# Scores' maxima placed behind the reciprocals of two Sinkhorn chains in VectorE's instruction order

## The chip, the core and the metric

The kernel runs on one core of a Trainium2 chip. The engines are TensorE (PE, with its weight loads shown apart as PEld), VectorE (DVE), ScalarE (ACT), GpSimd (POOL) and SyncE (SP, which issues the DMAs). Each of them takes its own instructions strictly in the order of its own list, and an instruction that waits holds up all that stand behind it in the same list. The metric is the device time of one execution in microseconds: before the change the median of three runs is 1359.68 us (1355.14 to 1362.71).

## The reference, cut to what matters

Two transformer layers with adaptive layer norm. The first (gated linear attention and a binarised feed-forward) fills about the first 900 us and is not touched. The second layer is a softmax attention (batch 2, 512 tokens each, 32 heads of 16), and then a feed-forward made of four streams, whose mixing matrices come from 50 rounds of a Sinkhorn normalisation for each of 1024 tokens:

```python
scores = einsum('bqhd,bkhd->bhqk', q, k) / sqrt(D)
probs  = softmax(scores)                       # needs a row's maximum
out    = einsum('bhqk,bkhd->bqhd', probs, v)
...
Z = (x_norm @ W_res.T + H_res_base) / tau      # a 4 x 4 matrix for each token
for _ in range(50):
    u = -logsumexp(Z + v[None, :], axis=-1)
    v = -logsumexp(Z + u[:, None], axis=-2)
H_res = exp(Z + u[:, None] + v[None, :])
...
x_mixed = einsum('btij,btjc->btic', H_res, x_streams)
```

## The kernel before

Tokens lie on the 128 partitions, so there are eight tiles of 128 tokens: four of batch 0 and four of batch 1.

**The attention of the second layer** is cut into 16 steps (batch, half of the queries, group of heads) of 8 pieces each. `piece()` emits, for one piece, `maxima(order[i], k)`, then the weighing of a piece that lies ten behind, then `aside(2)`. `maxima` writes two score tiles: a matmul (L880) into one of three PSUM banks, and a VectorE reduction (L884) that takes the negated maximum of each row and so frees the bank. That makes 256 maxima in all; they are counted here as maximum 1 to 256. After every four pieces the eight maxima are split in two parts (L894 on ScalarE, L895 on GpSimd), transposed, and sent into the queries' tile. `weigh` repeats the scores with the maxima subtracted (L918) and takes the exponential on ScalarE (tile `pt`, L78). `outputs` (L938) and `finish` (reciprocal L964, product L966 on VectorE, addition L972 on GpSimd) close one "quad" for every eight maxima.

**The Sinkhorn chains** are generators that `aside` advances two steps for each piece. As soon as two token tiles of the attention's output are complete, a chain begins:

- chain a (`streams0(0)`, tiles 0 and 1 of batch 0) and chain b (`streams0(2)`, tiles 2 and 3 of batch 0): 49 iterations each, whose products and sums run on GpSimd and whose reciprocals run on VectorE;
- the chain of batch 1, whose products, sums and reciprocals are all on VectorE (`last` is true): 16 iterations of the first two tiles alone, 33 of all four tiles together (the joint chain, 128x16 operands), and 16 of the last two tiles alone.

One half iteration of chain a or b is a round between two engines: a product on GpSimd (L1183 or L1187), two additions on GpSimd (L1176, L1177), a reciprocal on VectorE (L1185 or L1189), and then the product of the next half. At iterations 16 and 32 the kernel matrix is renewed from logarithms, with ScalarE in the round (L1193, L1166, L1167). `opening` comes before a chain (statistics, two products per tile on GpSimd for batch 0 in L1061 and L1062), `mixed_on_tensor` after it (diagonal matrices `dg` on ScalarE, matmuls L1236, product `fout` L1210 on VectorE, addition L1211 on GpSimd).

**The order of the lists** is made by a list scheduler from the dependencies and priorities, when the program is built; the text of the kernel gives only the dependencies. The kernel also adds dependencies that cost no semaphore and only fix the order of two instructions of one engine:

```python
order_only = mybir.DependencyInfo(mybir.DependencyClass.NoSync, mybir.DependencyReason.DATA)
tc.add_manual_dep(m, i.name, order_only, reason="the work beside keeps its place")
```

In the list built for VectorE before the change, 64 of chain a's 98 reciprocals and 28 of chain b's 98 stand ahead of maximum 256; the other 104 stand behind it.

Of the kernel before, what the change touches and what calls it, by code (L numbers as in the profile page):

```python
# [52 lines left out]
def tile_adaln(ctx: ExitStack, tc: tile.TileContext, a: dict, out: bass.AP):  # L53
    nc = tc.nc
# [22 lines left out]
    def act(o, i, func, **kw):  # L77
        ins = nc.scalar.activation(o, i, func, **kw)  # L78
        tc.add_manual_dep(
            ins.ins, table.ins.name,  # L80
            mybir.DependencyInfo(mybir.DependencyClass.NoSync, mybir.DependencyReason.DATA),
            reason="the activation table",
        )
        return ins.ins
# [52 lines left out]
    anchor = {}  # L137
    order_only = mybir.DependencyInfo(mybir.DependencyClass.NoSync, mybir.DependencyReason.DATA)
# [32 lines left out]
    def temp(shape, dt, name, bufs=2):  # L171
        return wk.tile(shape, dt, name=name, bufs=bufs)
# [642 lines left out]
    def key_tile(i):  # L815
        return i % 2 if i < TWO else (i - TWO + 2) % 3
# [54 lines left out]
    def maxima(st, k):  # L871

        assert holder[key_tile(st["i"])] == st["i"]
        rp, j = divmod(k, 4)
        s, i = divmod(j, 2)
        if j == 0:
            st["m"] = small.tile([P, NQ * 2, 2], FP, name="m")
        for qt in range(NQ):
            ps = psp.tile([P, L], FP, name="s1", bufs=S1)
            anchor["pe"] = nc.tensor.matmul(  # L880
                ps, lhsT=st["qs"][rp][0:KS, i, qt * P:(qt + 1) * P], rhs=st["ks"][s][0:KS],
                start=True, stop=True,
            ).ins
            anchor["dve"] = nc.vector.tensor_reduce(  # L884
                st["m"][:, 2 * qt + s, i:i + 1], ps, AX.X, ALU.max, negate=True
            ).ins
        if j == 3:
            m2 = small.tile([P, NQ * 2, 2, 2], FR, name="m2")
            hi, lo = m2[:, :, 0], m2[:, :, 1]
            if st is order[-1]:  # L890
                nc.vector.tensor_copy(hi, st["m"])
                nc.vector.tensor_tensor(lo, st["m"], hi.bitcast(FP), ALU.subtract)
            else:
                nc.scalar.copy(hi, st["m"])  # L894
                nc.gpsimd.tensor_tensor(lo, st["m"], hi.bitcast(FP), ALU.subtract)  # L895
            mt = psp.tile([8, Q], FP, name="mt", bufs=MT)
            for qt in range(NQ):
                nc.tensor.transpose(
                    mt[:, qt * P:(qt + 1) * P],
                    m2[:, 2 * qt:2 * qt + 2].bitcast(FP).rearrange("p a b c -> p (a b c)"), ident,  # L900
                )
            mm = temp([8, L], FR, "mm")[:, 0:Q]
            nc.scalar.copy(mm, mt)
            anchor["sp"] = nc.sync.dma_start(out=st["qs"][rp].bitcast(FP)[96:100], in_=mm.bitcast(FP)).ins

    def weigh(st, k):

        assert holder[key_tile(st["i"])] == st["i"]
        rp, r = divmod(k, 4)
        kp, s = divmod(r, 2)  # L910
        if r == 0:
            quads.append({"st": st, "rp": rp, "pt": {}})
        qd = quads[-1]
        for i in range(2):
            ps = psp.tile([P, 2, Q], FP, name="s2", bufs=S2)
            for j in range(2):
                kt = 2 * kp + j
                nc.tensor.matmul(  # L918
                    ps[:, j, :], lhsT=st["ks"][s][0:KM, kt * P:(kt + 1) * P], rhs=st["qs"][rp][0:KM, i, :],
                    start=True, stop=True,  # L920
                )
            p = wts.tile([P, 2, Q], FP, name="pt", bufs=PT)
            anchor["act"] = qd["last"] = act(p, ps, AF.Exp, scale=0.25)
            qd["pt"][2 * s + i, kp] = p

    quads = []

# [232 lines left out]
    def iterations(R, its, renew, last):  # L1160

        z, t, K, u, v, fa, fb, fl = (R[k] for k in ("z", "t", "K", "u", "v", "fa", "fb", "fl"))
        big = nc.vector if last else nc.gpsimd

        def kernel_of():
            nc.vector.tensor_tensor(K, z, over(u), ALU.add)  # L1166
            nc.vector.tensor_tensor(K, K, along(v), ALU.add)  # L1167
            act(K, K, AF.Exp)

        def sums(dst, y):  # L1170

            if last:
                nc.vector.tensor_reduce(dst, y, AX.X, ALU.add)  # L1173
            else:
                h2 = R["pairs"]
                nc.gpsimd.tensor_tensor(h2, y[:, :, :, 0:2], y[:, :, :, 2:4], ALU.add)  # L1176
                nc.gpsimd.tensor_tensor(dst, h2[:, :, :, 0], h2[:, :, :, 1], ALU.add)  # L1177

        for it in its:
            if it == 1 or it - 1 in renew:  # L1180
                sums(fa, K)
            else:
                big.tensor_tensor(t, K, along(fb), ALU.mult)  # L1183
                sums(fa, t)
            nc.vector.reciprocal(fa, fa)  # L1185
            yield
            big.tensor_tensor(t, tp_(K), along(fa), ALU.mult)  # L1187
            sums(fb, t)
            nc.vector.reciprocal(fb, fb)  # L1189
            if it in renew:  # L1190
                for d, f in ((u, fa), (v, fb)):
                    act(fl, f, AF.Ln)
                    nc.vector.tensor_tensor(d, d, fl, ALU.add)  # L1193
                kernel_of()
            yield
# [70 lines left out]
    def streams0(c0):  # L1266

        S = {"b": 0, "c0": c0, "n": 2}
        yield from opening(S, False)
        R = chain_room(2, False)  # L1270
        yield from first_iteration(S, R)
        yield from S["branch"]
        yield from iterations(R, range(1, NITER), RENEW, False)
        result(S, R)
        for c in range(2):
            yield from mixed_on_tensor(S, c, nc.gpsimd)
# [3 lines left out]
    def streams1a():  # L1280

        S = joint["a"] = {"b": 1, "c0": 0, "n": 2}
        yield from opening(S, True)
        R = joint["R"] = chain_room(4, True)
        yield from first_iteration(S, part(R, 0, 2))
        yield from S["branch"]
        yield from iterations(part(R, 0, 2), range(1, HEAD + 1), (HEAD,), True)

    def streams1b(ahead):
# [16 lines left out]

        side.append((1, branches(), UP))
        yield from iterations(R, range(1, NITER - HEAD), RENEW, True)
        result(A, part(R, 0, 2))
        side.append((None, mixed_on_tensor(A, 0, nc.gpsimd), UP))  # L1310
# [44 lines left out]
    def piece():  # L1355
        p = at[0]
        at[0] += 1
        if p == 0:
            begin()
        i, k = divmod(p, 8)  # L1360
        if k == 0 and i < len(order):
            load_step(i + 1)
        if p < n_pieces:
            maxima(order[i], k)
        if wt[0] <= p - slack(p):
            weighed()
        if k == 4 and i + 1 < len(order):
            keys1(i + 1)
        with tc.high_priority(UP):
            if p >= HOLD and p % POP == 0 and virtual:  # L1370
                tail(virtual.pop(0))
        aside(2)
# [3 lines left out]
    def weighed():  # L1376
        w = wt[0]
        wt[0] += 1
        if w < n_pieces:
            if w == n_pieces // 2:  # L1380
                values1(1)
            weigh(order[w // 8], w % 8)
        o = w - OUT
        if 0 <= o < n_pieces and o % 4 == 3:
            outputs(o // 4)
        o -= 5
        if o >= 0 and o % 4 == 0 and o < n_pieces:
            j = o // 4
            finish(j)
            if j % 16 == 5:  # L1390
                with behind():
                    row_tiles(j // 16, (SB, CB, GB))
                    weights24(j // 16)
            if j % 8 == 7:
                k = j // 8
                if k == 2:
                    joint["ahead"] = streams1a()
                side.append((RATES[k], (streams0(2 * k) if k < 2 else joint["ahead"] if k == 2 else streams1b(joint["ahead"])), UPS[k]))
# [40 lines left out]
    for n, u in enumerate(units):  # L1439
        g, b, c = u["at"]  # L1440
        s = n // NC
# [127 lines left out]
```

## Time and profile before

| What | Value |
|---|---|
| Median of three runs | 1359.68 us |
| The profiled execution, its own time | 1362.77 us |
| Its span in the trace | 1361.1 us |
| PE busy | 1236.3 us (91%) |
| DVE busy | 1098.5 us (81%) |
| ACT busy | 845.2 us (62%) |
| POOL busy | 788.3 us (58%) |
| Maximum 96, 192, 224 and 256 end at | 1057.5, 1165.3, 1195.4 and 1225.1 us |
| First reciprocal of chain a | 1081.1 us |
| Last addition of the attention's output (L966 of the last quad) | 1241 us |
| Joint chain, first and last reciprocal | 1256.2 and 1320.6 us |

An engine's busy share is an average over stages that have different limits. Three stages matter here: the attention while the chains run beside it (1081 to 1225 us), the rest of the attention with the openings of the last tiles (1225 to 1256 us), and the tail in which the chains alone are left (1256 to 1361 us).

### The profile page before, as it was taken

Reading aid. Unit: us, or ns where it says so; the run is one execution under the profiler, and the core shown is the slowest. Engines: PE = TensorE matmul, PEld = TensorE weight load, DVE = VectorE, ACT = ScalarE, POOL = GpSimd, SP = SyncE. Lnnn points to the kernel's source line nnn. Section 1 sums busy time; section 2 is a strip of 40 time slices with the busy share of each in tenths; the row PEclk is TensorE's granted clock in tenths of the full one; section 3 lists DMA queues with packets and bytes.
Section 4 is the critical chain, followed back from the end, with each engine's and each line's share of the span. In section 5 each row is a group of like instructions: output and inputs, shape, how many; then the busy total and the mean of one; then the engine's idle time right before and its main releaser. Section 6 shows DMA issues by size and latency. Waiting matters only on the chain. (4 is left out here: it accounts for less than half of the span.)

```text
span 1361.1 us, 23047 instructions
## 1 busy us (share of the span) xinstructions
PE 1236.3 (91%) x7216; PEld 996.9 (73%) x7216; DVE 1098.5 (81%) x2668; ACT 845.2 (62%) x2380; POOL 788.3 (58%) x1235
## 2 busy tenths in 40 slices
PE   6889999999999999999989999898999999995408
PEld 3677888788788778888877787676777777764308
DVE  7897678787686687877989887867878888898888
ACT  4565476476466566766657675566667678775417
POOL 5353374365266357776788878444444755668751
PEclk9999999999999999999999999998998999997659
DMA  8111341231132142333343233424203221200001
GB/s 255 57 57 32 97 121 40 71 109 55 46 95 93 54 139 95 86 108 93 101 125 109 82 113 91 127 71 132 81 28 116 81 68 50 66 14 2 9 8 47
DMA packets 69762, 109.68 MB, mean 81 GB/s; under 512 B 13436, under 2 KB 20348, under 8 KB 69640
## 3 DMA queue, kind: packets, MB, share of 16 engines
q1 hardware_dynamic: 69640, 108.21, 26.9%
q8 instruction: 57, 0.93, 0.3%
q14 instruction: 65, 0.53, 0.1%
HBM read 99.89 MB, written 8.02 MB: 79 GB/s over the span
## 5 line engine op out<-in xcount | busy, mean ns | idle before, releaser
L884 DVE TENSOR_REDUCE m<-s 128x1 f32<-128x512 f32 x256 | 165.7, 670 | 13.6 <-PE s L880 13.0
L78 ACT ACTIVATE pt<-s 128x512 f32<-128x512 f32 x256 | 137.6, 600 | 13.4 <-PE s L918 12.6
L78 ACT ACTIVATE sg<-sg 128x512 f32<-128x512 f32 x128 | 80.8, 632 | 57.9 <-DVE sg L512 56.0
L481 POOL TENSOR_TENSOR q<-xcos,rot 128x512 f32<-128x512 f32 x64 | 92.9, 1452 | 39.7 <-DVE xcos L479 36.9
L880 PE MATMUL s<-ks,qs 96*128 96x512 f32 x256 | 105.1, 438 | 8.4 <-DVE m L884 6.2
L251 PE MATMUL pps<-hh,wq_h 128*128 128x512 f32 x256 | 102.0, 399 | 0.9 <-DVE zl L605 0.9
L78 ACT ACTIVATE dec<-dec,room 128x128 f32<-128x128 f32 x256 | 82.7, 398 | 32.1 <-POOL dec L529 31.9
L529 POOL TENSOR_SCALAR_AFFINE_SELECT dec<-gb 128x512 f32<-128x512 f32 x64 | 47.1, 736 | 95.6 <-DMA gb<-g_dram 35.1
L251 PE MATMUL ops<-wo_h,zh 128*128 128x512 f32 x256 | 101.3, 396 | 0.9 <-DVE zl L605 0.9
L251 PE MATMUL ops<-wo_h,zl 128*128 128x512 f32 x256 | 100.8, 394 | 0.9 <-DVE zl L605 0.9
L251 PE MATMUL gps<-wg_h,hh 128*128 128x512 f32 x256 | 101.1, 395 | 0.0
L251 PE MATMUL gps<-wg_l,hh 128*128 128x512 f32 x256 | 101.0, 394 | 0.0
L918 PE MATMUL s<-qs,ks 100*128 100x256 f32 x512 | 99.3, 301 | 1.7 <-ACT pt L78 1.2
L251 PE MATMUL gps<-wg_h,hl 128*128 128x512 f32 x256 | 100.6, 393 | 0.0
L251 PE MATMUL pps<-hl,wq_h 128*128 128x512 f32 x256 | 100.3, 392 | 0.0
L251 PE MATMUL ops<-wo_l,zh 128*128 128x512 f32 x256 | 100.1, 391 | 0.0
L251 PE MATMUL pps<-hh,wq_l 128*128 128x512 f32 x256 | 100.1, 391 | 0.0
L549 POOL TENSOR_TENSOR gb<-gb,q 128x512 f32<-128x512 f32 x48 | 63.2, 1318 | 63.1 <-ACT gb L78 52.2
L582 PE MATMUL yps<-v,dec 128*128 128x128 f32 x512 | 93.8, 278 | 3.8 <-DVE xcos L479 2.8
L918 PEld LDWEIGHTS s<-qs,ks 100*128 100x128 f32 x512 | 83.0, 195 | 18.0 <-ACT pt L78 5.3
L592 DVE SCALAR_TENSOR_TENSOR z<-yps,ss,sg 128x128 f32<-128x128 f32 x256 | 71.8, 341 | 28.4 <-ACT ss L78 28.1
L556 POOL TENSOR_TENSOR xw<-v,room 128x512 f32<-128x512 f32 x48 | 55.5, 1171 | 60.4 <-ACT v L496 58.1
(327 smaller groups left out, 3924.5 us busy)
## 6 DMA issues: line engine op xcount, KB each, us to landing
gb<-g_dram SPq DMA_DIRECT2D x64, 256.0 KB
raw<-in_wq SPq DMA_DIRECT2D x56, 256.0 KB
raw<-in_wg SPq DMA_DIRECT2D x48, 256.0 KB
raw<-in_wo SPq DMA_DIRECT2D x48, 256.0 KB
raw<-in_wmod SPq DMA_DIRECT2D x40, 256.0 KB
qs<-q_dram SPq DMA_DIRECT2D x64, 64.0 KB
raw<-in_wk SPq DMA_DIRECT2D x14, 256.0 KB
raw<-in_wv SPq DMA_DIRECT2D x14, 256.0 KB
```

The costliest lines, as they stand in the source:

```text
L78: ins = nc.scalar.activation(o, i, func, **kw)
L251: nc.tensor.matmul(ps, lhsT=l, rhs=r, start=i == 0, stop=i == n - 1)
L481: nc.gpsimd.tensor_tensor(dst, sp(xc_), sp(rot), ALU.add)
L529: anchor["pool"] = nc.gpsimd.affine_select(out=dec, in_=gb, pattern=[[0, REP0], [1, P]], compare_op=ALU.is_ge, fill=-1e30, base=0, channel ...
L549: nc.gpsimd.tensor_tensor(gb, gb, q[:, c], ALU.mult)
L556: nc.gpsimd.tensor_tensor(xw, u["v"][:, c, :].unsqueeze(1).to_broadcast(sh4), wdc[:, c, r0:r0 + REP0].unsqueeze(2).to_broadcast(sh4), ALU. ...
L582: nc.tensor.matmul(yps[:, h, :], lhsT=u["pr"][:, h, :], rhs=u["v"][:, c, :], start=True, stop=not c)
L592: nc.vector.scalar_tensor_tensor(z[:, h, :], yps[:, h, :], ss[:, h:h + 1], sg[:, h * P:(h + 1) * P], ALU.mult, ALU.mult)
L880: anchor["pe"] = nc.tensor.matmul(ps, lhsT=st["qs"][rp][0:KS, i, qt * P:(qt + 1) * P], rhs=st["ks"][s][0:KS], start=True, stop=True,).ins
L884: anchor["dve"] = nc.vector.tensor_reduce(st["m"][:, 2 * qt + s, i:i + 1], ps, AX.X, ALU.max, negate=True).ins
L918: nc.tensor.matmul(ps[:, j, :], lhsT=st["ks"][s][0:KM, kt * P:(kt + 1) * P], rhs=st["qs"][rp][0:KM, i, :], start=True, stop=True,)
```

## The change

Every reciprocal of chains a and b is noted in a queue of its chain when it is emitted. Every maximum, when it is emitted, is given an order-only dependency on the oldest noted reciprocal of a chain: maxima of odd number on that of the oldest chain that has any left, maxima of even number on that of each of the first two chains that have any left. The chain of batch 1 is not noted. No instruction is added or removed, and no semaphore.

```diff
@@ maxima @@
             anchor["dve"] = nc.vector.tensor_reduce(
                 st["m"][:, 2 * qt + s, i:i + 1], ps, AX.X, ALU.max, negate=True
             ).ins
+            pace(anchor["dve"])
...
+    paced = {}
+    turn_ = [0]
+
+    def pace(m):
+
+
+        turn_[0] += 1
+        for q in [q for q in paced.values() if q][:1 if turn_[0] % 2 else 2]:
+            tc.add_manual_dep(m, q.pop(0).name, order_only, reason="the chain's reciprocals keep pace")
...
@@ iterations @@
-            nc.vector.reciprocal(fa, fa)
+            r = nc.vector.reciprocal(fa, fa).ins
+            if not last:
+                paced.setdefault(id(R), []).append(r)
             yield
             big.tensor_tensor(t, tp_(K), along(fa), ALU.mult)
             sums(fb, t)
-            nc.vector.reciprocal(fb, fb)
+            r = nc.vector.reciprocal(fb, fb).ins
+            if not last:
+                paced[id(R)].append(r)
```

## The prediction

> **What bounds the kernel now.** I read the slices of the page first, then the engines' busy time by stretch, then the maxima alone by stretch, and last the order of time around the chains.
>
> ```profile
> PE   6889999999999999999989999898999999995408
> DVE  7897678787686687877989887867878888898888
> ```
>
> PE is full until slice 36 and half empty after it: there is an attention that PE fills, and a tail in which it hardly works.
>
> ```profile
> core 0: us, PE busy (x) PEld busy (x) DVE busy (x) ACT busy (x) POOL busy (x), PEclk, DMA share, GB/s
> 1081.00:1165.00 84.00, 81.69 (x727) 62.19 (x728) 73.69 (x208) 68.56 (x168) 50.16 (x166) 0.96 0.24 64
> 1165.00:1195.00 30.00, 30.00 (x283) 23.11 (x281) 25.46 (x77) 22.54 (x56) 21.51 (x94) 1.00 0.27 62
> 1195.00:1225.00 30.00, 29.35 (x263) 20.33 (x267) 28.76 (x106) 23.35 (x60) 17.32 (x81) 1.00 0.04 10
> 1225.00:1256.00 31.00, 17.18 (x171) 12.60 (x162) 27.24 (x180) 16.93 (x50) 25.48 (x115) 0.81 0.01 2
> 1256.00:1321.00 65.00, 16.69 (x96) 15.33 (x95) 56.03 (x282) 17.01 (x62) 43.13 (x196) 0.61 0.02 9
> ```
>
> From 1081 to 1225 us PE is the bound (141 of 144 us) with VectorE close behind; from 1256 us on VectorE is (56 of 65 us), working on the joint chain, which reads tiles that the attention completes last.
>
> ```profile
> core 0: us, DVE busy (x), PEclk, DMA share, GB/s
> 1081.00:1165.00 84.00, 57.69 (x90) 0.96 0.24 64
> 1165.00:1195.00 30.00, 20.39 (x33) 1.00 0.27 62
> 1195.00:1225.00 30.00, 21.19 (x33) 1.00 0.04 10
> ```
>
> These are the maxima alone: 0.93, 0.91 and 0.91 us for each. That pace is to be compared with the chains' own.
>
> ```profile
> 1313.34 0.25 POOL L1187 TENSOR_TENSOR sinkhorn<-sinkhorn 128x32 f32<-128x32 f32 x1 [0.32 <-DVE sinkhorn L1185]
> 1313.67 0.22 POOL L1176 TENSOR_TENSOR sinkhorn<-sinkhorn 128x16 f32<-128x16 f32 x1
> 1313.96 0.20 POOL L1177 TENSOR_TENSOR sinkhorn<-sinkhorn 128x8 f32<-128x8 f32 x1
> 1314.48 0.24 POOL L1183 TENSOR_TENSOR sinkhorn<-sinkhorn 128x32 f32<-128x32 f32 x1 [0.32 <-DVE sinkhorn L1189]
> ```
>
> Here chain b is alone on GpSimd: product to product takes 1.14 us, of which 0.82 is three operations and 0.32 GpSimd's idling for the reciprocal. It is a closed round, and no shorter one of a single chain stands in the attention either (1.13 us).
>
> ```profile
> 1108.46 0.19 DVE L1189 RECIPROCAL sinkhorn<-sinkhorn 128x8 f32<-128x8 f32 x1
> 1108.57 1.24 DVE L884 TENSOR_REDUCE m<-s 128x1 f32<-128x512 f32 x2
> 1109.35 0.20 POOL L1177 TENSOR_TENSOR sinkhorn<-sinkhorn 128x8 f32<-128x8 f32 x1
> 1109.73 0.20 DVE L964 RECIPROCAL rc<-ot 128x8 f32<-128x8 f32 x1
> 1109.84 0.64 DVE L884 TENSOR_REDUCE m<-s 128x1 f32<-128x512 f32 x1
> 1110.40 0.19 DVE L1185 RECIPROCAL sinkhorn<-sinkhorn 128x8 f32<-128x8 f32 x1
> ```
>
> This is what the change alters: chain a's sums are ready at 1109.55, and its reciprocal comes only at 1110.40, behind three maxima. Today the chain waits for the maxima; 42 reciprocals (22 and 20 in the stretch's rows) go through in 84 us, one in 2.0 us.
>
> **The change part by part.** No instruction is added. In the list built for VectorE, 179 reciprocals of chains a and b now stand ahead of maximum 256 (98 of a, 81 of b) where 92 did; 17 are left behind it instead of 104. Maxima 97 to 192 have exactly one reciprocal of a before each ("a, m, a, m"), and from 163 on 30 of b's besides; maxima 193 to 224 have 17 of b's among them, 225 to 256 have 34. The lists of the first layer stay the same but for the start, which I take as nothing (within 2 us either way). Since the lists are kept in order, a reciprocal that waits for GpSimd now holds the next maximum, that holds its PSUM bank, the matmul of L880 waits for one of three banks, and the weighing behind it in PE's list waits too: ScalarE's exponentials and the quads come later with it.
>
> *Start.* Chain a's first reciprocal came at 1081.1 with six maxima between 96 and it; they now stand behind (6 x 0.67 = 4.0 us of VectorE). Between 1077 and 1081, as the stretch is partly a chain of short steps: I take 1079.
>
> *Maxima 97 to 192.* A round of a is at least 1.14 us. The maximum hides in it: it starts 0.11 after the reciprocal and takes 0.67, which leaves 0.36. For every eight maxima a quad brings L964 and L966 (0.19 + 0.27 = 0.46, so 0.10 too much) and on GpSimd L972 and L895 (0.46 + 0.20) between the rounds: 0.76 for eight, so 1.24 us for each; 96 x 1.24 = 119.0. GpSimd's long operations stop the round whole: three of L708 and two of L702 (3 x 1.27 + 2 x 1.68 = 7.2), and b's opening, two each of L1061 and L1062 (1.38, 1.28) and two pairs of L134 and L135 (0.19 + 0.71): 7.1. Each of a's two renewals takes longer than a round: today's has reciprocals at 1148.19 and 1152.05, 3.86 - 1.14 = 2.7, twice 5.4. With b beside it both chains took a product each per 1.34 us (1263.93 to 1266.61 for two halves): 30 x 0.10 = 3.0. Sum 119.0 + 14.3 + 5.4 + 3.0 = 141.7, so maximum 192 ends at 1220.7 instead of 1165.3. Bounds: 96 x 1.14 + 5.4 = 114.8 if all else hides, 96 x (1.34 + 0.10) + 19.7 = 158 if a keeps the pace of two chains all along.
>
> *Maxima 193 to 224.* Few reciprocals bind; they keep their 30 us: 1250.7.
>
> *Maxima 225 to 256.* 34 x 1.14 = 38.8, with b's second renewal (2.7) and four quads (3.0): 44.5 instead of 29.7, so 1295.2. Bounds 38.8 and 51 (34 x 1.34 and the rest).
>
> *PE's cover.* PE's work is about 0.9 us for a maximum and lies under 1.24. The rows show a granted clock of 0.81 when PE was 55% busy and 0.96 to 1.00 when full; 0.91 / 0.81 = 1.12 stays under it.
>
> The Trainium skill, "TensorE: Matmul & The Clock Gate", section "A second HAM failure mode: psum-queue depth-cycling", speaks against the change: where PE idles for moments between bursts because of PSUM banks, the clock swings between half and full. As an estimate, half of the time at half clock would make 0.91 into 1.21 us, still hidden; always at half, 1.82 us and some 55 us more for 96 maxima.
>
> *The tail*, 1225.1 to 1361.1 = 136.0 us now, is what pays. Most of it stays: the last quads (to 1241), the last tiles' opening and first iteration (to 1256), the joint chain, 16 iterations that already run at VectorE's own 1.38 us, the mixing. Gone are 65 reciprocals that stood among the joint chain's operations (131 of L1185 and L1189 between 1256 and 1321, less its own 66). One costs its slot of 0.12 us when it is ready, 0.24 alone; as VectorE idles only 9 of 65 us there, I take the slot: 7.8 us. Two `fout` products of chain a go forward into the attention: each cost 0.6 us and stretched a product beside GpSimd's addition from 0.21 to 1.25, so 3.3. The tail becomes 124.9 us (116.9 with 0.24; 136 if nothing comes of it).
>
> *Sum.* 1295.2 + 124.9 = 1420.1 us of span. The profiled time lies 1.7 above its span, and the median 3.1 below that: 1419 us, 4.3% more.
>
> **The rivals.**
>
> *The rounds run at their floor.* Everything beside them hides: 1077 + 114.8 + 30 + 38.8 + 124.9 = 1385.5, so 1384. For it: b kept 1.14 beside a loaded VectorE. Against it: no stretch of today's attention keeps it for two rounds running.
>
> *Queues hold each other.* A reciprocal waits for GpSimd, GpSimd for L895's cast on ScalarE (4.5 us of such waits between 1081 and 1165), that for the maximum behind the reciprocal: 1079 + 158 + 30 + 51 + 136 = 1454, so 1453.
>
> *The tail falls faster than the attention grows.* The joint chain would be paced by the reciprocals queued among its operations, not by VectorE: their removal gives 65 x 0.24 = 15.6, the idle 9 and the 3.3, 28 us. It decides once the attention grows by less than 28 us, that is, once the two stalls above (55 and 15) are mostly covered; with 15 us of growth the time is 1347. Against it: 96 rounds of 1.14 from 1077 end at 1186 or later, 21 us after today, and 34 more add 9; the sum exceeds 28 before anything else.
>
> *The change does nothing*, because the scheduler places the reciprocals early anyway: 1360. The counts 92 and 179 exclude it nearly.
>
> **How the numbers follow.** Forecast 0.72, floor 0.12, queues 0.09, faster 0.05, nothing 0.02. Differences under 0.5% (6.8 us) can't be told from none with this kernel. The range reaches from just under the floor's time to the queues' time, 1380 to 1453; faster 0.05, same 0.02, slower 0.93.
>
> **What would show it.** Right: maxima 97 to 192 take 115 us or more, VectorE's idle time ends on L1177 (before reciprocals) rather than on L880 (before maxima), PE's L880 waits for L884 by tens of us, chains a and b have all but a few reciprocals before the last maximum, the joint chain runs alone in under 58 us. Wrong: maximum 192 before 1190 us, or a joint chain under 50 us.

## The result, and the profile after

The changed kernel takes 1425.31 us (median of five runs, 1423.27 to 1427.21) where the one before took 1360.78 us beside it: a ratio of 1.0477, 95% interval 1.0454 to 1.0500. Forecast were 1419 us and 1.043. The profiled execution has a span of 1423.7 us.

| Stage, by the traces | before, us | forecast, us | after, us |
|---|---|---|---|
| Chain a's first reciprocal, at | 1081.1 | 1079 | 1076.5 |
| from there to the end of maximum 192 | 84.2 | 141.7 | 142.7 |
| maxima 193 to 224 | 30.1 | 30 | 38.2 |
| maxima 225 to 256 | 29.7 | 44.5 | 45.9 |
| the tail, to the end | 136.0 | 124.9 | 120.4 |
| span | 1361.1 | 1420.1 | 1423.7 |

The second row holds 90 maxima before the change (103 to 192) and 96 after it (97 to 192). Stages are better compared by their lengths than by the time at which they end: maximum 96, behind which the change begins to act, ends at 1057.5 us in the trace before, at 1054.1 us in the trace after, and between 1052.4 and 1056.4 us in eleven traces of the experiments, whatever the kernel.

First the busy time by stretch in the changed kernel, cut where these stages end (columns as in the same view of the kernel before):

```profile
1076.00:1219.00 143.00, 116.95 (x789) 73.46 (x788) 97.85 (x302) 75.58 (x185) 98.69 (x414) 0.81 0.14 40
1219.00:1257.00 38.00, 37.18 (x339) 29.68 (x338) 29.12 (x82) 29.71 (x86) 20.67 (x76) 1.00 0.20 60
1257.00:1303.00 46.00, 40.62 (x313) 26.74 (x311) 39.89 (x177) 28.11 (x74) 25.65 (x111) 0.89 0.03 9
1303.00:1327.00 24.00, 12.23 (x112) 8.07 (x110) 16.66 (x94) 11.54 (x31) 15.60 (x58) 0.77 0.01 1
1327.00:1385.00 58.00, 18.82 (x124) 17.79 (x124) 49.24 (x208) 20.19 (x73) 2.54 (x2) 0.65 0.03 10
```

In the first row no engine is full: PE 82%, VectorE 68%, GpSimd 69%. Before the change PE had filled that stage. Where no engine is full, something that they wait for in turn sets the pace; the order of time on VectorE shows a round with GpSimd (start, duration, operation; in brackets how long the engine had been idle and what ended that):

```profile
1112.05 0.64 DVE L884 TENSOR_REDUCE m<-s 128x1 f32<-128x512 f32 x1
1112.66 0.21 DVE L975 RECIPROCAL rc<-ot 128x8 f32<-128x8 f32 x1
1113.06 0.20 DVE L1196 RECIPROCAL sinkhorn<-sinkhorn 128x8 f32<-128x8 f32 x1 [0.19 <-POOL sinkhorn L1188]
1113.18 0.64 DVE L884 TENSOR_REDUCE m<-s 128x1 f32<-128x512 f32 x1
...
1116.53 0.20 DVE L1202 RECIPROCAL sinkhorn<-sinkhorn 128x8 f32<-128x8 f32 x1 [0.38 <-POOL sinkhorn L1188]
1116.65 0.64 DVE L884 TENSOR_REDUCE m<-s 128x1 f32<-128x512 f32 x1
1117.65 0.20 DVE L1196 RECIPROCAL sinkhorn<-sinkhorn 128x8 f32<-128x8 f32 x1 [0.37 <-POOL sinkhorn L1188]
1117.77 0.64 DVE L884 TENSOR_REDUCE m<-s 128x1 f32<-128x512 f32 x1
```

One reciprocal, one maximum, every 1.13 us (1112.05 to 1113.18) and 1.12 us (1116.65 to 1117.77). The maximum starts 0.12 us after the reciprocal, and VectorE then idles until GpSimd's second addition (L1188 here, L1177 before) is done. A quad's reciprocal (L975) fits into that idle time. The waits of VectorE between 1076 and 1303 us (engine and line, whom it waited for, us in total, times, longest) have turned round accordingly: before the change it waited 11.2 us for PE before maxima and 3.9 us for GpSimd.

```profile
DVE sinkhorn L1196 <- POOL sinkhorn L1188: 19.1, 39, 2.6
DVE sinkhorn L1202 <- POOL sinkhorn L1188: 15.9, 42, 0.9
DVE m L884 <- PE s L880: 9.6, 11, 1.7
```

And PE, which waited 1.0 us for VectorE's maxima before, now waits for what hangs on them (between 1080 and 1303 us); the first row is the DMA that puts the split maxima into the queries' tile:

```profile
PE s L919 <- DMA qs<-mm: 9.6, 8, 2.6
PE s L880 <- DVE m L884: 8.6, 15, 1.7
```

### The profile page after: what moved, and what is told of

The parts are those of the page before. It is cut to its first block, busy times and chain, and to the rows that moved or that the text cites. A ratio compares the mean times of both kernels' runs of the same rounds, so it can differ in the third digit from the quotient of the medians.

```text
span 1423.7 us, 23048 instructions
## 1 busy us (share of the span) xinstructions
PE 1271.7 (89%) x7216; PEld 1003.2 (70%) x7216; DVE 1112.7 (78%) x2668; ACT 846.1 (59%) x2380; POOL 790.5 (56%) x1235
## 5 line engine op out<-in xcount | busy, mean ns | idle before, releaser
L884 DVE TENSOR_REDUCE m<-s 128x1 f32<-128x512 f32 x256 | 165.8, 662 | 11.0 <-PE s L880 10.9
L880 PE MATMUL s<-ks,qs 96*128 96x512 f32 x256 | 111.3, 468 | 18.8 <-DVE m L884 13.6
L919 PEld LDWEIGHTS s<-qs,ks 100*128 100x128 f32 x512 | 82.4, 204 | 32.4 <-issue 11.8
L1251 PE MATMUL mix<-h,dg 128*128 128x128 f32 x224 | 37.4, 321 | 64.0 <-ACT dg L1230 64.0
```

The costliest lines, as they stand in the source:

```text
L880: anchor["pe"] = nc.tensor.matmul(ps, lhsT=st["qs"][rp][0:KS, i, qt * P:(qt + 1) * P], rhs=st["ks"][s][0:KS], start=True, stop=True,).ins
L884: anchor["dve"] = nc.vector.tensor_reduce(st["m"][:, 2 * qt + s, i:i + 1], ps, AX.X, ALU.max, negate=True).ins
L919: nc.tensor.matmul(ps[:, j, :], lhsT=st["ks"][s][0:KM, kt * P:(kt + 1) * P], rhs=st["qs"][rp][0:KM, i, :], start=True, stop=True,)
L1251: nc.tensor.matmul(mps[:, i], lhsT=dg[:, j], rhs=hv[:, j] if j < NS else yb[:, c], start=n > NS and j == 0, stop=j == n - 1 and (n > NS or ...
```

## The experiments

Each of the twelve runs is compared with the kernel before the change on the same chip. "Maximum 256 at" and the like come from the traces.

**A shorter round in the changed kernel.** In `sums` of chains a and b:

```diff
-                nc.gpsimd.tensor_tensor(h2, y[:, :, :, 0:2], y[:, :, :, 2:4], ALU.add)
-                nc.gpsimd.tensor_tensor(dst, h2[:, :, :, 0], h2[:, :, :, 1], ALU.add)
+                nc.gpsimd.tensor_tensor(dst, y[:, :, :, 0], y[:, :, :, 1], ALU.add)
```

> The changed kernel with one GpSimd addition in place of two in the sums of chains a and b (half of each sum is left out, so the output is another). Theory: the round falls by the slot of that addition, 0.29 us, for the 96 maxima of a and the 34 of b that are paced by it: 130 x 0.29 = 38 us off, 1387 us, bounds 1380 to 1400 (VectorE's and PE's own pace of 0.9 us stops it). Rival (the growth comes of waits on ScalarE, DMAs and quads): under 10 us off, over 1415 us.

Measured: 1394.61 us, ratio 1.0252 (1.0232 to 1.0272), 31 us less. From chain a's first reciprocal to maximum 192 it took 118.6 us instead of 142.7, maxima 225 to 256 took 36.6 instead of 45.9. The maxima alone, by stretch:

```profile
1077.00:1196.00 119.00, 61.63 (x96) 0.91 0.16 48
1196.00:1232.00 36.00, 20.94 (x33) 1.00 0.21 61
1232.00:1269.00 37.00, 20.86 (x33) 1.00 0.05 14
```

The same 96 maxima, 61.6 us of work as in the changed kernel, come in 119 us: 24.1 / 96 = 0.25 us less for each, of the 0.29 that left the round.

**The same edit before the change**, as a control.

> The kernel before the change with one GpSimd addition in place of two in the sums of chains a and b (half of each sum is left out): the control to the same edit of the changed kernel, which took 31 us off it. Theory (before the change the attention does not wait for the rounds): maximum 256 stays at 1220 to 1228 us, some 14 more reciprocals ahead of it, 1353 to 1362 us. Rival (the addition costs GpSimd time that counts anyway): 1345 us or less.

Measured: 1360.76 us, ratio 0.9999 (0.9984 to 1.0014), maximum 256 at 1222.3 us. The addition costs nothing where no maximum waits for the round. With the run before this shows that the round paces the changed kernel's attention.

**Half the pace.** Every second maximum is left free:

```diff
-        for q in [q for q in paced.values() if q][:1 if turn_[0] % 2 else 2]:
+        for q in [q for q in paced.values() if q][:0 if turn_[0] % 2 else 2]:
```

> Only every second maximum stands behind a reciprocal (of each of the first two chains); the others are free. Theory (a maximum that must follow each round of a chain is slowed to the round's 1.14 to 1.24 us): one round for two maxima (1.82 us at PE's pace) hides, so the attention ends as before the change (maximum 256 at 1225 to 1233), 41 more reciprocals than before stand ahead of it, which takes 41 x 0.12 = 5 us off the tail: 1350 to 1362 us. Rival (any such placement makes queues hold each other, whatever its rate): most of the growth stays, over 1390 us.

Measured: 1376.68 us, ratio 1.0132 (1.0111 to 1.0152), between the two. From maximum 113 to 160 the pace is that before the change (each 16 take 13.7 to 14.1 us against 13.6 to 13.8); the 16 before them, at chain a's start, take 41.0 instead of 37.9. Maxima 161 to 192 then take 41.1 us instead of 28.8, maxima 225 to 256 take 36.9 instead of 29.7. GpSimd's and VectorE's order of time at the first of these places:

```profile
1136.26 2.88 POOL L1072 TENSOR_TENSOR h<-h,row 128x512 f32<-128x512 f32 x2
1139.25 2.53 POOL L1073 TENSOR_TENSOR h<-h,row 128x512 f32<-128x512 f32 x2
```

```profile
1140.37 0.69 DVE L884 TENSOR_REDUCE m<-s 128x1 f32<-128x512 f32 x1 [0.40 <-PE s L880]
1142.40 0.20 DVE L1196 RECIPROCAL sinkhorn<-sinkhorn 128x8 f32<-128x8 f32 x1 [1.33 <-POOL sinkhorn L1188]
...
1149.80 0.20 DVE L1165 RECIPROCAL sinkhorn<-sinkhorn 128x8 f32<-128x8 f32 x1
...
1150.96 0.19 DVE L1196 RECIPROCAL sinkhorn<-sinkhorn 128x8 f32<-128x8 f32 x1
1151.07 0.64 DVE L884 TENSOR_REDUCE m<-s 128x1 f32<-128x512 f32 x1
```

The GpSimd rows are chain b's opening (L1061 and L1062 before the change). Chain a's round stands still behind them, until 1142.40, and then goes on. Maximum 164 nevertheless starts 10.7 us after maximum 163 (1140.37 to 1151.07): it is the first that stands behind a reciprocal of b, and that one (1150.96) needs the whole opening and b's first iteration (whose reciprocal is L1165). So the rate was forecast rightly, but the order allows no lateness: a maximum tied to a chain that is only starting waits for the start. Neither side of the expectation held as a whole.

**A milder pace with room to be late.** Every second maximum, behind the oldest chain alone, and only while that chain has more than six reciprocals noted:

```diff
-        for q in [q for q in paced.values() if q][:1 if turn_[0] % 2 else 2]:
+        for q in [q for q in paced.values() if len(q) > 6][:0 if turn_[0] % 2 else 1]:
```

> A milder pace: every second maximum stands behind a reciprocal of the oldest chain that has more than six noted, so the chain may be six reciprocals late. Theory (a stop of GpSimd is paid only where the pace leaves no slack): maximum 256 at 1225 to 1232 us, 118 reciprocals ahead of it instead of 92, 26 x 0.12 = 3 us off the tail: 1354 to 1364 us, no better than before the change. Rival (any pace costs): over 1370 us.

Measured: 1365.93 us, ratio 1.0051 (1.0033 to 1.0069). That is just over the theory's range. Maximum 224 comes at 1196.4 us (1195.4 before the change), but maximum 96 had come 5.0 us earlier in this trace; from 96 to 224 it takes 143.9 us instead of 137.9. Most of that is in maxima 161 to 176, at chain b's start: 19.8 us, where the kernel before takes 15.0 and half the pace took 27.8. The room to be late makes the stop smaller and does not remove it. Maxima 225 to 256 take 35.9 us, and the tail 131.4 instead of 136.0. The list shows what was moved there: 11 reciprocals of batch 1's own chain stand ahead of maximum 256 instead of 2.

**The same up to maximum 224 only.**

```diff
         turn_[0] += 1
+        if turn_[0] > 224:
+            return
```

> The milder pace (every second maximum behind a reciprocal of the oldest chain with more than six noted) for maxima up to 224 only; in the run with that pace to the end maxima 225 to 256 had taken 36 us instead of 30. Theory (VectorE's and PE's work is only moved between attention and tail): maximum 256 at 1222 to 1228, 104 reciprocals ahead of it instead of 92, 12 x 0.12 = 1.4 us off: 1355 to 1361 us, the same as before the change. Rival (some order of this kind beats it): under 1352 us.

Measured: 1365.39 us, ratio 1.0039 (1.0022 to 1.0056); maximum 256 at 1224.8 us, the profiled span 1361.6 us. By the timed runs it is a little slower than expected, and from maximum 96 to the end the trace takes 306.9 us instead of 303.5 (maxima 161 to 176 again 19.8 instead of 15.0). None of the orders tried beat the kernel before.

**The oldest chain alone at full pace.**

```diff
-        for q in [q for q in paced.values() if q][:1 if turn_[0] % 2 else 2]:
+        for q in [q for q in paced.values() if q][:1]:
```

> Every maximum stands behind a reciprocal of the oldest chain alone. Theory: maxima 97 to 192 as in the changed kernel (142 us, b runs beside unpaced); from 193 on b has 33 reciprocals to do for 64 maxima instead of 51, so 3 to 12 us less there; more of b's (36 instead of 17) is left for the tail, 19 x 0.12 = 2 us more: 1412 to 1424 us. Rival (the second dependency is what costs most of the growth): under 1395 us.

Measured: 1417.29 us, ratio 1.0417 (1.0390 to 1.0445). From chain a's first reciprocal to maximum 192 it takes 142.1 us, as in the changed kernel; maxima 225 to 256 take 29.9. The second dependency costs 16 us in that last stretch, and its reciprocals give some of that back in the tail (130.4 us instead of 120.4). The total lies in the theory's range, but by two sizes that were both too small: from maximum 193 on it saves 17 us, not 3 to 12, and the tail is 10 us longer, not 2.

**Chain b alone at full pace.** Chain a is not noted:

```diff
+        if c0:
+            paced[id(R)] = []
...
-            if not last:
-                paced.setdefault(id(R), []).append(r)
+            if not last and id(R) in paced:
+                paced[id(R)].append(r)
```

> The changed kernel with chain b alone noted: maxima up to 160 are free, from 161 on each stands behind a reciprocal of b, with chain a beside it unpaced. Theory: maximum 160 comes at 1137 us as before the change, then 96 x (1.34 to 1.44) + 5.4 = 134 to 144 us, so maximum 256 at 1271 to 1281, and a tail of some 120: 1391 to 1402 us. Rival (the growth is mainly GpSimd's long operations and the start of chain a, which fall before maximum 160): under 1380 us.

Measured: 1430.72 us, ratio 1.0521 (1.0503 to 1.0539), worse than the changed kernel with fewer maxima paced. Maximum 160 comes at 1132.6 us, as expected, so it is not the time before it that matters. But the next 96 maxima take 164.5 us, not 134 to 144. The list has chain a's reciprocals between b's all the same (64 of a ahead of maximum 192, 97 ahead of maximum 224), so each maximum stands behind two rounds:

```profile
1215.24 0.64 DVE L884 TENSOR_REDUCE m<-s 128x1 f32<-128x512 f32 x1
1215.98 0.20 DVE L1202 RECIPROCAL sinkhorn<-sinkhorn 128x8 f32<-128x8 f32 x1
1216.43 0.20 DVE L1196 RECIPROCAL sinkhorn<-sinkhorn 128x8 f32<-128x8 f32 x1 [0.25 <-POOL sinkhorn L1188]
1216.55 0.64 DVE L884 TENSOR_REDUCE m<-s 128x1 f32<-128x512 f32 x1
```

1.31 us from maximum to maximum is what two chains need on GpSimd, near the 1.34 used in the forecast. The stretch's mean is higher, 1.89 and 1.77 us for maxima 161 to 192 and 193 to 224, with GpSimd busy 47 of 60 and 46 of 57 us. One part of the rest is again chain b's start: maximum 161, the first that stands behind a reciprocal of b, starts 14.5 us after maximum 160 (at 1146.46 us), and the theory had no term for that. The remainder was not taken apart.

**The tail without the two chains.** Before the change, with both cut where the last maximum finds them:

```diff
-        yield from iterations(R, range(1, NITER), RENEW, False)
+        yield from iterations(R, range(1, 15 if c0 else 33), RENEW, False)
```

> The kernel before the change with chain a cut after 32 iterations and chain b after 14 (17 and 35 iterations left out), as many as stand ahead of the last maximum there: the tail without their reciprocals and without the attention's growth. Theory (VectorE's own work paces the joint chain): 104 reciprocals at 0.12 us and four fout products forward at 1.65 us: 12.5 + 6.6 = 19 us off at most, 11 by the rows of the joint chain alone, so 1342 to 1350 us. Rival (the reciprocals' waits pace the joint chain): 28 us and more off, under 1333 us.

Measured: 1359.58 us, ratio 0.9999 (0.9986 to 1.0011): no gain at all, which neither side expected. The joint chain did shrink, from 64.4 to 55.3 us, that is by 9.1 us for 65 reciprocals (0.14 each, near the slot of 0.12). But the last quad (the end of its product L966, which the table of the kernel before calls an addition) came 33.8 us after maximum 256 instead of 16.4. ScalarE's groups between 1222 and 1256 us show what stands there (count, busy us, mean ns), and the busy time by stretch that PE and ScalarE are both full (32.94 and 32.83 of 34 us):

```profile
L1215 ACT ACTIVATE dg<-room,sinkhorn 128x128 f32<-128x128 f32 x60 | 19.0, 386 | 0.0
L78 ACT ACTIVATE pt<-s 128x512 f32<-128x512 f32 x16 | 8.3, 575 | 0.0
L1215 ACT ACTIVATE dg<-room,sm 128x128 f32<-128x128 f32 x13 | 5.0, 385 | 0.0
```

```profile
1222.00:1256.00 34.00, 32.94 (x300) 27.93 (x289) 23.75 (x116) 32.83 (x106) 5.16 (x6) 1.00 0.07 25
```

Chains that end early bring their mixing early: 24 us of it stand on ScalarE among the last 16 exponentials, on which the last quads wait, and its matmuls on PE. That the mixing delays the quads is a reading so far; the next run tests it.

**The same with the mixing behind the last quad.** The mixing is emitted only after the last weighing, and each `dg` has an order-only dependency on the last `os`:

```diff
+        while wt[0] < n_pieces + OUT + 5:
+            yield
...
+                    if i.engine == joint["os"].engine:
+                        tc.add_manual_dep(i, joint["os"].name, order_only, reason="behind the last quad")
```

> As the run with both chains cut (a after 32 iterations, b after 14), but the diagonal matrices of their mixing stand behind the last quad's copy on ScalarE. In the run before it the joint chain took 55.3 us (64.5 before the change), yet the last quad came 33 us after maximum 256 (16 before the change). Theory (the mixing, brought forward, delays the last quads on ScalarE and PE and eats the tail's gain): the last quad comes again 14 to 18 us behind maximum 256, the joint chain stays at 55 to 58 us, 1344 to 1352 us. Rival (something else delays the quads, or the mixing then delays the joint chain by as much): 1357 us or more.

Measured: 1354.53 us, the median of nine executions, ratio 0.9962 (0.9944 to 0.9979). The tenth, the one that was profiled, took 2475.57 us, so where the stages end is not known. The time lies between the two sides: the mixing's place is worth 5 us, while the quads had been 17 us late. Whether they came in time here, and what else holds the tail, stays open. With 52 of 98 iterations left out, and so no reciprocal of the two chains in the tail, the whole kernel gains these 5 us and no more.

**The mixing late in the changed kernel.** The same edit in it.

> The changed kernel with the diagonal matrices of the mixing of chains a and b behind the last quad's copy on ScalarE. In the changed kernel maxima 193 to 224 took 38 us (30 before the change), with 40 matmuls of a's mixing among them. Theory (chain a's mixing, brought into the attention, takes PE's and ScalarE's time there): they take 30 to 33 us, the tail gets two fout products back (3.3 us): 1418 to 1424 us with maximum 256 at 1295 to 1299. Rival (PE has weighing to catch up there, whatever the mixing): they still take 36 us or more, 1425 us or more.

Measured: 1421.22 us, ratio 1.0443 (1.0416 to 1.0470), with maxima 193 to 224 in 33.2 us instead of 38.2 and maximum 256 at 1296.4. In the changed kernel PE did 11.8 us of `mix` in that stretch (its line alone; the 80 records are two for each of 40 matmuls), which the late mixing takes out of it (the maxima alone, in the other kernel):

```profile
1219.00:1257.00 38.00, 11.80 (x80) 10.86 (x80) 1.00 0.20 60
```

```profile
1219.00:1252.00 33.00, 20.33 (x33) 1.00 0.21 63
```

The theory held in the stretch, nearly to its upper bound. VectorE's list shows a second way in which the early mixing held the maxima, which no run separates from PE's work: a `fout` product (L1225) stood among them and waited for `mix` (1219 to 1257 us; with the late mixing no such wait is left):

```profile
DVE fout L1225 <- PE mix L1251: 3.5, 2, 2.9
```

The 4 us between the totals are not separated from no difference, since the intervals overlap.

**A longer lag of the weighing.**

```diff
-LAG = 10
+LAG = 12
```

> The changed kernel with the weighing twelve pieces behind the maxima in place of ten. In the changed kernel PE's L919 waited 9.6 us for the DMA that puts the maxima into the queries' tile, which it did not before. Theory (the paced maxima set the rate, these waits fill time that PE has anyway): no gain, and two more pieces behind the last maximum, 1422 to 1432 us. Rival (the waits for the DMA are part of the growth): 1416 us or less.

Measured: 1419.08 us, ratio 1.0431 (1.0398 to 1.0464), between the two sides; the interval overlaps the changed kernel's. PE's waits between 1080 and 1297 us:

```profile
PE s L880 <- DVE m L884: 16.0, 23, 1.8
...
PE s L919 <- DMA qs<-mm: 1.0, 1, 1.0
```

The waits for the DMA are gone, 9.6 to 1.0 us, and the waits for the maxima have grown from 8.6 to 16.0 in their place. From maximum 96 to the end the trace takes 367.0 us instead of 369.6. That is how a wait looks that mostly fills time.

**PE kept busier.** A second score matmul over half of the keys for maxima 97 to 192:

```diff
+            if 48 <= 8 * st["i"] + k < 96:
+                nc.tensor.matmul(
+                    ps[:, 0:Q], lhsT=st["qs"][rp][0:KS, i, qt * P:(qt + 1) * P], rhs=st["ks"][s][0:KS, 0:Q],
+                    start=True, stop=True,
+                )
```

> The changed kernel, with each score matmul of maxima 97 to 192 led by a second one over half of the keys into the same bank (overwritten, so the output stays): more work for PE where it idles. In the changed kernel the granted clock was at half for 55 of the 143 us of these maxima, where one took 1.71 us, and 1.14 in the full-clock stretches 1104 to 1124 and 1135 to 1148. Theory (the half clock is part of what a paced maximum costs): with PE busier the granted clock stays above 0.9, maxima 97 to 192 take 125 to 134 us instead of 143, 1408 to 1418 us. Rival (the half clock only fills time in which the round, GpSimd's long operations and the renewals hold the maxima anyway): the clock rises, but the stretch stays at 140 us or more, 1421 us or more. If the clock does not rise, it stays open.

Measured: 1424.84 us, ratio 1.0482 (1.0460 to 1.0505), and 143.1 us from chain a's first reciprocal to maximum 192. The clock rose less than wanted; the stretch by engines:

```profile
1077.00:1219.00 142.00, 120.00 (x862) 82.91 (x864) 97.16 (x301) 75.62 (x184) 99.15 (x411) 0.86 0.14 41
```

0.86 instead of 0.81, some 14 us less at half clock, bought nothing. That speaks for the rival, but the added work may have eaten a small gain, so what the half clock costs here is bounded, not settled.

## Why the prediction was right

**The bound.** "A reciprocal that waits for GpSimd now holds the next maximum" is what the trace shows at 1.13 us, and the two runs with the shorter round show that this, and not the reciprocals' own time, is the cost.

**Maxima 97 to 192**: 141.7 forecast, 142.7 measured. The sum is right, but not every term of it. The quads' 0.10 us for each maximum (96 x 0.10 = 10 us) was too much: in the full-clock stretch at 1112 us the round stays at 1.13 with a quad in it. What took its place are single stops: maxima 111, 135 and 151 come 3.4 to 3.8 us after the one before, after waits of 1.0 to 1.5 us for PE. Where PE's clock is at half the mean rises to 1.7 us for a maximum (6 in 10 us from 1125 on), but the round itself does not slow: maxima 130 to 132 stand in that stretch and come every 1.13 to 1.14 us; the rest is a wait of 1.8 us for GpSimd at its start and one of 1.0 us for PE at its end. In the whole stage (1077 to 1219 us) VectorE's waits for PE are 5.0 us before maxima and 2.6 before quads' reciprocals, against 33.1 us for GpSimd before the chains' reciprocals. So by direct waits PE, at whatever clock, holds VectorE for 7.6 of the 142.7 us; what it costs in other ways the last run leaves open. "PE's cover" was thinner than written: PE was busy 117 / 96 = 1.22 us for each of these maxima, not 1.12.

**The start.** Forecast 1079, measured 1076.5. That is partly chance: 3.4 of the 4.6 us by which chain a begins earlier are those by which maximum 96 came earlier.

**The Trainium skill's rule** ("TensorE: Matmul & The Clock Gate", section "A second HAM failure mode: psum-queue depth-cycling") is that PE, idling for moments between groups of matmuls while it cycles through PSUM banks, has its clock swing between half and full. The trace agrees as to the swing. Before the change the granted clock was 1.00 from 1090 to 1225 us, with PE busy 134.35 of 135 us; in the changed kernel neighbouring stretches have these granted clocks (the column before the last two):

```profile
1104.00:1124.00 20.00, 18.59 (x141) 12.05 (x138) 14.75 (x44) 11.83 (x27) 11.58 (x51) 0.99 0.10 28
1125.00:1135.00 10.00, 7.58 (x46) 3.71 (x44) 5.09 (x14) 3.29 (x9) 5.48 (x25) 0.50 0.08 23
1135.00:1148.00 13.00, 11.52 (x88) 7.84 (x84) 9.07 (x26) 8.77 (x21) 8.17 (x36) 1.00 0.12 34
```

A mean of 0.81 over 143 us is 54 us at half clock if only these two values occur: less than the middle case that the prediction worked out from the page (half of the time). The other case, always at half, did not come. That the waits for PSUM banks, and not PE's other waits, bring the swing about is not shown.

**Maxima 193 to 224**: 30 forecast, 38.2 measured. The step "they keep their 30 us" is the one that failed: chain a now ends here, and its mixing comes with it. The prediction moved that mixing out of the tail and costed it at nothing in the attention, where PE was 98% busy; with the mixing behind the last quad the stretch took 33.2 us. The other 3 us were not taken apart.

**Maxima 225 to 256**: 44.5 and 45.9.

**The tail**: 124.9 and 120.4. The joint chain gave 6.0 us for its 65 reciprocals (7.8 forecast; 9.1 in the run with the chains cut), what follows it 2.1 (3.3 forecast). Not forecast are the 7.4 us between maximum 256 and the joint chain (31.1 to 23.7). There the rows of L1185 and L1189 count 67 reciprocals before the change and those of L1196 and L1202 count 27 after it: 23 reciprocals of batch 1's own chain, instead of 2, had already been done while the attention waited. The sum left that out. That these reciprocals are the whole of the 7.4 us is read from the rows and not tested. (The prediction's lower value for the tail is off in itself: 136.0 - 15.6 - 3.3 is 117.1, not 116.9.)

**The sum.** The total is nearer than its terms, and that is luck: 2.5 us at the start and 4.5 in the tail are too long, 1.0, 8.2 and 1.4 us in the three stages of the attention too short, which leaves 3.6 us of span. Another 3 us are the last step, from the span to the median: the profiled execution before lay 3.1 us above its median, the one after does not (1425.47 against 1425.31 us).

**The signs named.** VectorE's idle time ends on GpSimd's addition (35.0 us) rather than on L880 (9.6 us), and 179 of 196 reciprocals stand ahead of the last maximum, as named. Two signs did not come: PE's L880 waited 8.6 us for L884, not tens of us, and the joint chain took 58.4 us, not under 58. What slows PE besides is the wait for the DMA behind the maxima (9.6 us) and a longer busy time of its own, 116.95 us for 96 maxima where 81.69 had gone with 90.

**The rivals.** The floor (1384) is out, as stops and renewals do not hide, nor do the queues hold each other to the extent of 1453. The tail did not fall faster than the attention grew: 15.6 us were gained for 78 lost, and the runs with the chains cut show that even without their reciprocals it offers some 5 us as the kernel stands. That the change does nothing was excluded by the counts in the list, rightly.

## What to carry to other kernels

Before an instruction is placed behind another one in an engine's list, look at what that other one waits for: if it is part of a round between two engines, the round's time becomes the least pace of all that is queued behind it, here 1.14 us against 0.91. An order that ties each step pays every long operation of the other engine and the start of the chain that it is tied to; one that lets the round fall behind by a few steps pays less of it (19.8 us against 27.8 for the same 16 maxima, 15.0 without any order), not nothing. And work that is brought forward brings its successors along, so cost them where they land.

## What the runs showed of the hardware

- The granted clock of PE alternated between half and full in the changed kernel, and PE's busy share in a stretch does not tell which: 7.58 of 10 us (from 1125 us) and 2.97 of 3 us (from 1200 us) were busy at 0.50, 18.59 of 20 us (from 1104 us) at 0.99 and 11.52 of 13 us (from 1135 us) at 1.00.
- Two chains of 128x32 products and additions on GpSimd take 1.31 us for a round of both, six operations, where one chain alone needs 1.13 to 1.14 us for three. An operation that needs the result of the one before starts 0.29 to 0.33 us after it (1313.34, 1313.67 and 1313.96 us); one of the other chain starts 0.16 to 0.20 us after it (1215.37, 1215.54, 1215.74 and 1215.90 us with chain b paced).
